# Ten batches of an MLP turned by VectorE blocks and SBUF transfers in place of TensorE transposes

## The chip, the cores and the metric

The kernel runs on one core of a Trainium2 chip. The metric is the device time of one execution in microseconds, and the median over the runs counts.

## The reference

The reference is one transformer block over 16 batches of 256 tokens with 256 features: modulated layer norm and self-attention with 16 heads, cross-attention to a context of 256 tokens, and an MLP of width 1024. All of it is fp32.

```python
x = x + gate_a[:, None] * attn_out          # self-attention
x = x + c_attn_out                          # cross-attention
x_norm2 = modulate(_ln(x), shift_m, scale_m)   # _ln(x) * (1 + scale_m) + shift_m
h = jax.nn.gelu(x_norm2 @ W_mlp1 + b_mlp1)
h = h @ W_mlp2 + b_mlp2
x = x + gate_m[:, None] * h
```

The change touches only the MLP's input: `x_norm2` must have the features on the partitions before it is multiplied by `W_mlp1`.

## The kernel before

The attention of all batches comes first and takes most of the time. It writes its result `x` to a DRAM tensor (`X2d`). The MLP then goes through the batches in order. Some of its first batches begin beside the end of the attention; from batch 3 on a loop at the end of the program (L1209 to L1234) drives it, and this loop is the place of the change.

Each matrix product is made of three fp32r products. Every operand is split into a rounded part (hi) and the rest (lo), and hi x hi, hi x lo and lo x hi are summed in PSUM.

A batch of the MLP goes in these steps:

- `mlp_load` (L804) reads `x` of the batch from DRAM, by SP's queue. `mlp_bias` (L812) adds the cross-attention's bias on GpSimd. `mlp_stats` (L815) takes mean and variance on VectorE, `pow` (L307) makes the reciprocal root on GpSimd, and `mlp_apply` (L819) writes the normalized rows `xn` on VectorE, tokens on partitions, in two instructions of 128x256.
- `mlp_T` (L833) turns `xn` by four TensorE transposes of 128x128 into PSUM (`psT_m`). VectorE scales and shifts them into SBUF (`xTf_m`, two instructions), ACT writes the same, rounded, to hi (two instructions), and VectorE subtracts hi to get lo. hi and lo lie in `Wkc` for even batches and `Wqc` for odd ones (`wkch`, `wkcl`, `wqch`, `wqcl` in the profile); these are weight tiles of the attention that are no longer needed.
- The width of 1024 is cut into four chunks c of 256. `mlp_first` (L857) makes one chunk in PSUM (`ph`, twelve matmuls of 128x256). `mlp_gelu` (L890) reads `ph` on ACT twice, once for the exact value `hf` and once for the rounded `hh` (two instructions each), and GpSimd subtracts them to `hl`. `mlp_second` (L907) multiplies the chunk by `W_mlp2` into PSUM (`st` or `s`, by the batch's parity; twelve matmuls) over all four chunks. After the last chunk VectorE multiplies by the gate (`mt`), adds the residual (`y`), and SP stores it.
- `mlp_gates` (L822) loads the gate's rows (`gm`), and `mlp_residual` (L828) prepares `xmg` on VectorE.

One turn of the loop is one chunk (b, c), and the text calls it so. TensorE gets, in this order: at c = 0 the four transposes of batch b+1, then `mlp_first` of the chunk two ahead, then `mlp_second` of the chunk before. So in (b, 0) it works on `ph` of (b, 2) and the last chunk of batch b-1, and `ph` of (b+1, 0), the first that needs hi and lo of batch b+1, comes in (b, 2).

The order on TensorE, VectorE, GpSimd and SP is the program's order (`keep_in_program_order`, L52); only ACT is left to a scheduler in the last part. Every instruction goes through the helper at L51, so nearly all rows of the profile have that line, and are told apart by their tiles.

Of the kernel before, what the change touches and what calls it, by code (L numbers as in the profile page):

```python
# [10 lines left out]
F32 = mybir.dt.float32  # L11
F32R = mybir.dt.float32r
AF = mybir.ActivationFunctionType
ALU = mybir.AluOpType
AX = mybir.AxisListType

P = 128
# [4 lines left out]
def pixart_block(  # L22
# [8 lines left out]
    B, N, H = x.shape  # L31
# [3 lines left out]
    NT = N // P  # L35
    KC = H // P
# [21 lines left out]
    ACT, DVE, POOL, SP = (InOrder(e, True) for e in (nc.scalar, nc.vector, nc.gpsimd, nc.sync))  # L58

    const = ctx.enter_context(tc.tile_pool(name="const", bufs=1))  # L60
    work = ctx.enter_context(tc.tile_pool(name="work", bufs=2))
# [6 lines left out]
    def ps_gen(name, tag=None):  # L68


        if tag is None and ps_turn[0] is not None:
            ps_turn[0] ^= 1
            tag = (SHORT, LONG)[ps_turn[0]]
        tag = tag or SHORT
        return psum.tile([P, 512], F32, tag=tag, name=name, bufs=2)
# [25 lines left out]
    def tok(ap, b):  # L101
        return ap[b].rearrange("(t p) h -> p t h", p=P)
# [18 lines left out]
    def wtile(name, c):  # L121
        return [const.tile([P, KC, c], F32R, name=f"{name}{s}") for s in ("h", "l")]

    Wq, Wk, Wv, Wp = [[wself[:, 4 * i:4 * i + 2], wself[:, 4 * i + 2:4 * i + 4]] for i in range(4)]
    Wqc = wtile("wqc", H)
    Wkc, Wvc, Wcp = wtile("wkc", H), wtile("wvc", H), wtile("wcp", H)
    cpT = const.tile([P, 12, B], F32, name="cpT")
    bqkv = const.tile([P, 6, B], F32, name="bqkv")
    sc1 = const.tile([P, 2, 2, B], F32, name="sc1")
    bT = const.tile([P, 32], F32, name="bT")  # L130
# [302 lines left out]
    def mm3_tok(dst, xT, t, W, kn=KC, start=True, stop=True):  # L433
        n = 0
        for k in range(kn):
            for a, b in ((xT[0], W[0]), (xT[0], W[1]), (xT[1], W[0])):
                PE.matmul(dst, a[:, k, t * P:(t + 1) * P], b[:, k],
                          start=(start and n == 0), stop=(stop and n == 3 * kn - 1))
                n += 1
# [134 lines left out]
    def bc_t(ap):  # L574
        return ap.unsqueeze(1).to_broadcast([P, NT, H])
# [113 lines left out]
    def side(home, r):  # L689
        return home[r] if isinstance(home, (list, tuple)) else home[:, r]  # L690
# [111 lines left out]
    M = {}  # L802

    def mlp_load(b):  # L804
        m = M[b] = M.get(b) or Box()
        if not hasattr(m, "h"):
            m.h, m.hT, m.kept = {}, {}, []
        m.xt = work.tile([P, NT, H], F32, tag="x" if b > 1 else "c", name=f"x2_{b}", bufs=5 if b > 1 else 2)
        SP.dma_start(m.xt, tok(X2d, b))
        m.ln = layernorm(lambda: m.xt, f"m{b}")  # L810

    def mlp_bias(b):  # L812
        POOL.tensor_tensor(M[b].xt, M[b].xt, bc_t(cb), ALU.add)

    def mlp_stats(b, power=False):  # L815
        M[b].ln.steps[0]()
        M[b].ln.steps[1](power)

    def mlp_apply(b):  # L819
        M[b].ln.steps[2]("dve")  # L820

    def mlp_gates(b):  # L822
        m = M[b]
        m.g = work.tile([P, 2, H], F32, tag="g", name=f"gm_{b}", bufs=3)
        SP.dma_start(m.g.rearrange("p a h -> p (a h)"),
                     gd[b, 2:4].rearrange("a h -> (a h)").partition_broadcast(P))

    def mlp_residual(b):  # L828
        m = M[b]
        m.xg = work.tile([P, NT, H], F32, tag="x1", name=f"xmg_{b}", bufs=7)  # L830
        DVE.tensor_tensor(m.xg, m.xt, bc_t(m.g[:, 1]), ALU.add)

    def mlp_T(b):  # L833

        m = M[b]
        pst = ps_gen(f"psT_m{b}", SHORT)
        for f in range(KC):
            for t in range(NT):
                PE.transpose(pst[:, f * N + t * P:f * N + (t + 1) * P],
                             m.ln.xn[:, t, f * P:(f + 1) * P], ident)  # L840
        y = work.tile([P, KC, N], F32, tag="y", name=f"xTf_m{b}", bufs=2)
        hi, lo = (Wkc, Wqc)[b % 2]
        for f in range(KC):
            DVE.tensor_scalar(y[:, f], pst[:, f * N:(f + 1) * N], sc1[:, 1, f, b:b + 1],
                              cpT[:, 6 + f, b:b + 1], ALU.mult, ALU.add)
        if b in E_['DV']:
            DVE.tensor_copy(hi, y)
        else:
            for f in range(KC):
                ACT.activation(hi[:, f], pst[:, f * N:(f + 1) * N], AF.Identity,  # L850
                               bias=cpT[:, 6 + f, b:b + 1], scale=sc1[:, 1, f, b:b + 1])
        DVE.tensor_tensor(lo, y, hi, ALU.subtract)
        m.xT = (hi, lo)

    NCH = NF // 2

    def mlp_first(b, c):  # L857

        ph = ps_gen(f"ph_{b}_{c}", LONG).rearrange("p (j n) -> p j n", j=2)
        for j in range(2):  # L860
            mm3(ph[:, j], W1, 2 * c + j, M[b].xT)
        M[b].h[c] = ph
# [27 lines left out]
    def mlp_gelu(b, c):  # L890
        ph = M[b].h.pop(c)
        homes = (("pt", 5), ("qkh", 3), ("qkl", 3))
        if b == 0 and c:
            homes = (("x1", 7),) + (homes[1:] if c < 3 else (("xTh", 5), ("xTl", 5)))
        hf, hh, hl = [work.tile([P, 2, N], t, tag=tag, name=f"{n}_{b}_{c}", bufs=bufs)
                      for n, t, (tag, bufs) in zip(("hf", "hh", "hl"), (F32, F32R, F32R), homes)]
        for dst in (hf, hh):
            if c in M[b].kept:
                ACT.activation(dst, ph, AF.Gelu_apprx_tanh)
                continue  # L900
            for j in range(2):
                f = BM1 + 2 * c + j
                ACT.activation(dst[:, j], ph[:, j], AF.Gelu_apprx_tanh, bias=bT[:, f:f + 1])
        POOL.tensor_tensor(hl, hf, hh, ALU.subtract)
        M[b].hT[c] = (hh, hl)

    def mlp_second(b, c):  # L907
        m = M[b]
        hT = m.hT.pop(c)
        if c == 0:  # L910
            m.po = [side((st, sp)[b % 2], t)[:, :H] for t in range(NT)]
        done = c == NCH - 1
        if done:
            t1 = work.tile([P, NT, H], F32, tag="t1", name=f"mt_{b}")
            y = work.tile([P, NT, H], F32, tag="x1", name=f"y_{b}", bufs=7)
        for t in range(NT):
            mm3_tok(m.po[t], hT, t, [W2[0][:, 2 * c:2 * c + 2], W2[1][:, 2 * c:2 * c + 2]],
                    kn=2, start=(c == 0), stop=done)
            if done and b == B - 1:
                DVE.tensor_tensor(t1[:, t], m.po[t], m.g[:, 0], ALU.mult)  # L920
                DVE.tensor_tensor(y[:, t], m.xg[:, t], t1[:, t], ALU.add)
                SP.dma_start(tok(out, b)[:, t], y[:, t])
        if done and b < B - 1:
            for t in range(NT):
                DVE.tensor_tensor(t1[:, t], m.po[t], m.g[:, 0], ALU.mult)
            DVE.tensor_tensor(y, m.xg, t1, ALU.add)
            SP.dma_start(tok(out, b), y)
# [6 lines left out]
    steps = {"x": mlp_load, "b": mlp_bias, "s": mlp_stats, "p": lambda b: M[b].ln.pow(), "a": mlp_apply,  # L934
             "r": mlp_residual, "g": mlp_gates, "T": mlp_T, "F": lambda j: mlp_first(j // NCH, j % NCH),
             "G": lambda j: mlp_gelu(j // NCH, j % NCH), "S": lambda j: mlp_second(j // NCH, j % NCH)}

    def tail_word(w):
# [96 lines left out]
    for i in range(3):  # L1035
        b = i if i < 2 else 0
        u = ahead_of_mlp(nu + i, b)
        u.T, u.ln = [], []
        if i < 2:
            u.ln = [layernorm(lambda b=b: M[b].xt, f"m{b}")]  # L1040
            u.T = [transposed(lambda u=u: u.ln[0].xn, f"m{b}", [sc1[:, 1, f, b:b + 1] for f in range(KC)],
                              bias=[cpT[:, 6 + f, b:b + 1] for f in range(KC)])]
# [153 lines left out]
    last, o, q = units[-1], units[-1].post, units[-2].post  # L1196
    chunks = [(b, c) for b in range(B) for c in range(NCH)]
    M[0].h[3] = tail[2].K.ps.rearrange("p (j n) -> p j n", j=2)
# [9 lines left out]
        done[w]() if w in done else tail_word(w)  # L1208
    for i, (b, c) in list(enumerate(chunks))[12:]:  # L1209
        ACT.on = i < E_['AP']  # L1210
        if i + 1 < len(chunks):
            mlp_gelu(*chunks[i + 1])
        if c == 0 and b < B - 1:
            mlp_T(b + 1)
        if i + 2 < len(chunks):
            mlp_first(*chunks[i + 2])
        mlp_second(*chunks[i - 1])
        ahead = b + 2 if b + 2 < B else None
        if c == 0 and ahead:
            mlp_bias(ahead)  # L1220
        if c == 1:
            if b + 1 < B:
                mlp_gates(b + 1)
            if ahead:
                mlp_stats(ahead)
            if b + 3 < B:
                mlp_load(b + 3)
        if c == 2 and ahead:
            M[ahead].ln.pow()
        if c == 3:  # L1230
            if ahead:
                mlp_apply(ahead)
            mlp_residual(b)
    mlp_second(*chunks[-1])  # L1234


# [46 lines left out]
```

## Time and profile before

| | before |
|---|---|
| median of 3 runs | 743.66 us (741.77 to 743.85) |
| profiled execution, its own time | 741.67 us |
| its span | 739.3 us |
| TensorE busy (PE) | 732.6 us, 99% |
| VectorE busy (DVE) | 572.3 us, 77% |
| ACT busy | 564.0 us, 76% |
| GpSimd busy (POOL) | 540.0 us, 73% |
| granted TensorE clock | 1.00 |

In the profile PE is TensorE's matmuls, PEld its weight loads, DVE is VectorE, POOL is GpSimd, and SPq is the queue of transfers that SyncE issues. A row of the timeline has the start and the length in us from the start of the span, the engine, the line, the operation, the tile written and the tiles read, their shapes, the number of instructions merged into the row, and in brackets the idle time of the engine before it and what ended it. A row of the chain of waits has the start, the length and the work that the end of the program hung on at that time. A row of the groups has the operation, the count, and behind the bar the busy time in us, the mean in ns of one instruction, and the idle time before them. The MLP's loop fills the span from about 560 us on.

### The profile page before, as it was taken

Reading aid. Unit: us, or ns where it says so; the run is one execution under the profiler, and the core shown is the slowest. Engines: PE = TensorE matmul, PEld = TensorE weight load, DVE = VectorE, ACT = ScalarE, POOL = GpSimd, SP = SyncE. Lnnn points to the kernel's source line nnn. Section 1 sums busy time; section 2 is a strip of 40 time slices with the busy share of each in tenths; the row PEclk is TensorE's granted clock in tenths of the full one; section 3 lists DMA queues with packets and bytes.
Section 4 is the critical chain, followed back from the end, with each engine's and each line's share of the span. In section 5 each row is a group of like instructions: output and inputs, shape, how many; then the busy total and the mean of one; then the engine's idle time right before and its main releaser. Section 6 shows DMA issues by size and latency. Waiting matters only on the chain.

```text
span 739.3 us, 25308 instructions
## 1 busy us (share of the span) xinstructions
PE 732.6 (99%) x10152; PEld 648.9 (88%) x10152; DVE 572.3 (77%) x1187; ACT 564.0 (76%) x979; POOL 540.0 (73%) x571
## 2 busy tenths in 40 slices
PE   9999999999999999999999999999999999999997
PEld 9878888888888888888888888888889999999997
DVE  4788898988889898888889898888726656666662
ACT  3278898888888888888888888898886666666663
POOL 6776687969687696968769798798647766666553
PEclk9999999999999999999999999999999999999999
DMA  6755445443544445354445545545113122221311
GB/s 193 214 151 152 132 129 141 128 131 93 170 120 135 135 135 145 95 160 130 133 136 147 154 124 163 137 142 150 58 61 106 51 72 71 61 86 44 86 51 37
DMA packets 89065, 87.98 MB, mean 119 GB/s; under 512 B 8626, under 2 KB 84692, under 8 KB 88948
## 3 DMA queue, kind: packets, MB, share of 16 engines
q1 hardware_dynamic: 88484, 85.58, 41.2%
q8 instruction: 80, 1.31, 0.7%
q0 software_dynamic: 192, 0.52, 0.3%
q14 instruction: 37, 0.30, 0.1%
q10 hardware_dynamic: 272, 0.26, 0.1%
HBM read 26.97 MB, written 8.46 MB: 48 GB/s over the span
## 4 chain that ended last, share of the span: by engine, by line
PE 95%; POOL 1%; DVE 1%; ACT 1%; issue 1%; DMA 0%; SPq 0%; POOLq 0%; ACTq 0%
PE s L51 18%; PE o L51 16%; PE st L51 16%; PE ph L51 11%; PE ps_q L51 5%; PE ps_qc L51 4%; PE ps_v_c L51 3%; PE ps_kc L51 3%; PE ps_P_s L51 3%; PE ps_k L51 3%; PE ps_P_c L51 2%; PE ps_v_s L51 2%; PE psT_q L51 1%; PE psT_m L51 1%; PE ps_h L51 1%; PE psA_s L51 1%
## 5 line engine op out<-in xcount | busy, mean ns | idle before, releaser
L51 DVE TENSOR_REDUCE mx<-s 128x2 f32<-128x512 f32 x504 | 324.6, 683 | 64.2 <-PE s L51 58.1
L51 ACT ACTIVATE pt<-st 128x1024 f32<-128x1024 f32 x252 | 258.9, 1027 | 16.6 <-PE st L51 10.5
L51 PE MATMUL s<-big 63*128 63x256 f32 (+1 forms) x1024 | 183.6, 297 | 0.1
L51 PEld LDWEIGHTS s<-big 63*128 63x128 f32 (+1 forms) x1024 | 133.3, 185 | 18.3 <-DVE l_kc L51 6.6
L51 PE MATMUL st<-big 64*128 64x256 f32 (+1 forms) x1024 | 134.3, 298 | 0.6 <-DMA big<-m 0.3
L51 POOL TENSOR_TENSOR hl<-hf,hh 128x512 fp32r<-128x512 f32 x64 | 84.9, 1329 | 64.6 <-ACT hh L51 64.6
L51 PE MATMUL o<-pt,v 128*32 128x256 f32 x2048 | 123.8, 382 | 0.0
L51 PEld LDWEIGHTS st<-big 64*128 64x128 f32 (+1 forms) x1024 | 96.0, 186 | 16.4 <-issue 13.2
L51 PEld LDWEIGHTS o<-pt,v 128*32 128x32 f32 x2048 | 60.0, 109 | 41.4
L51 ACT ACTIVATE hf<-ph,bT 128x256 f32<-128x256 f32 x114 | 47.8, 473 | 27.6 <-PE ph L51 27.6
L51 ACT ACTIVATE hh<-ph,bT 128x256 fp32r<-128x256 f32 x114 | 47.8, 471 | 22.5 <-PE s L51 11.8
L51 ACT COPY oT<-o 128x512 f32<-128x512 f32 x63 | 36.9, 586 | 33.2 <-PE o L51 33.2
L51 DVE TENSOR_SCALAR xn_m<-x,mv_m,rs_m 128x256 f32<-128x256 f32 x28 | 24.0, 900 | 32.1 <-POOL rs_m L51 32.1
L51 PE MATMUL st<-big,hh 128*128 128x256 f32 x256 | 46.7, 281 | 0.0
L51 PE MATMUL s<-big,hh 128*128 128x256 f32 x256 | 46.7, 281 | 0.0
L51 PE MATMUL ph<-wkch,wself 128*128 128x256 f32 x224 | 44.9, 284 | 0.0
L51 PE MATMUL ph<-wqch,wself 128*128 128x256 f32 x224 | 44.7, 284 | 0.0
L51 PE MATMUL ps_k<-xTh_s,wself 64*128 64x256 f32 (+1 forms) x232 | 43.7, 294 | 0.0
L51 POOL TENSOR_SCALAR xn_c<-c,mv_c,rs_c 128x256 f32<-128x256 f32 x32 | 38.9, 1226 | 1.7
L51 PE MATMUL ps_q<-xTh_s,wself 64*128 64x256 f32 (+1 forms) x240 | 39.7, 282 | 0.0
L51 PEld LDWEIGHTS s<-big,hh 128*128 128x128 f32 x256 | 39.0, 188 | 0.0
L51 PEld LDWEIGHTS st<-big,hh 128*128 128x128 f32 x256 | 39.0, 188 | 0.0
(244 smaller groups left out, 2517.1 us busy)
## 6 DMA issues: line engine op xcount, KB each, us to landing
big<-h_kc SPq DMA_DIRECT2D x64, 128.0 KB
big<-h_qc SPq DMA_DIRECT2D x64, 128.0 KB
big<-h_k SPq DMA_DIRECT2D x62, 128.0 KB
big<-h_q SPq DMA_DIRECT2D x62, 128.0 KB
big<-l_k SPq DMA_DIRECT2D x32, 128.0 KB
big<-l_q SPq DMA_DIRECT2D x32, 128.0 KB
g<-gd SPq DMA_DIRECT2D x16, 256.0 KB
c<-in_ctx_dram SPq DMA_DIRECT2D x16, 256.0 KB
```

The lines of the kernel that those rows point to most:

```text
L51: i = f(*a, **k)
```

## The change

For batches 6 to 15 (`TURN = 6`) TensorE no longer turns the rows. VectorE turns `xn` in blocks of 32x32 into a tile `z`, in two instructions. Four transfers on SP's queue, 64 KB each in runs of 512 bytes from SBUF to SBUF, then bring the blocks to their partitions in a tile `y` (`yT` in the profile). VectorE scales and shifts `y` back into `z` (two instructions), copies it rounded to hi, and subtracts to get lo. ACT no longer writes hi. The tokens of these batches come out in another order (block of 32, half, token in the block); GELU writes its result back in the old order, so the later steps see no difference.

So that the transfers have time, the steps of these batches are moved forward in the loop: the load to (b, 0) for batch b+3, the bias to (b, 2), the statistics to (b, 3) behind the residual, the reciprocal root of batch b+2 to (b, 0), the normalization and the turn to (b, 1). The scaling, copy and subtraction of batch b+1 stand in (b, 0), where the transposes stood. The lists of instructions of the two programs differ on TensorE in ten groups of four transposes that are gone, and in nothing else.

```diff
+    TURN = 6
+
+    def mlp_turn(b):
+        m = M[b]
+        m.z = work.tile([P, 4, KC, NT * 32], F32, tag="xn", name=f"z_{b}", bufs=3)
+        m.y = work.tile([P, 4, KC, NT * 32], F32, tag="y", name=f"yT_{b}", bufs=2)
+        for t in range(NT):
+            DVE.transpose(m.z[:, :, :, 32 * t:32 * t + 32].rearrange("p j k c -> p k j c"),
+                          m.ln.xn[:, t].rearrange("p (k c j) -> p k j c", k=KC, j=4))
+        for a in range(4):
+            SP.dma_start(m.y[:, a].rearrange("p k c -> p (k c)"),
+                         m.z[32 * a:32 * a + 32].rearrange("r j k c -> r j (k c)"))
+
+    def mlp_turned(b):
+        m = M[b]
+        hi, lo = m.xT = (Wkc, Wqc)[b % 2]
+        for f in range(KC):
+            DVE.tensor_scalar(m.z[:, :, f], m.y[:, :, f], sc1[:, 1, f, b:b + 1],
+                              cpT[:, 6 + f, b:b + 1], ALU.mult, ALU.add)
+        y = m.z.rearrange("p a k c -> p k a c")
+        hi, lo = [w.rearrange("p k (a c) -> p k a c", a=4) for w in (hi, lo)]
+        DVE.tensor_copy(hi, y)
+        DVE.tensor_tensor(lo, y, hi, ALU.subtract)
...
-                ACT.activation(dst[:, j], ph[:, j], AF.Gelu_apprx_tanh, bias=bT[:, f:f + 1])
+                src, to = ph[:, j], dst[:, j]
+                if b >= TURN:
+                    src = src.rearrange("p (a t c) -> p a t c", a=4, t=NT)
+                    to = to.rearrange("p (t a c) -> p a t c", a=4, t=NT)
+                ACT.activation(to, src, AF.Gelu_apprx_tanh, bias=bT[:, f:f + 1])
...
+        by_dma = [d if d < B and d >= TURN else None for d in range(b + 1, b + 4)]
+        by_pe = b + 2 if b + 2 < TURN else None
+        if c == 0 and by_dma[1]:
+            M[by_dma[1]].ln.pow()
         if i + 1 < len(chunks):
             mlp_gelu(*chunks[i + 1])
-        if c == 0 and b < B - 1:
-            mlp_T(b + 1)
+        if c == 0 and b + 1 < B:
+            (mlp_turned if by_dma[0] else mlp_T)(b + 1)
+        if c == 0 and by_dma[2]:
+            mlp_load(by_dma[2])
...
         if c == 1:
+            if by_dma[1]:
+                mlp_apply(by_dma[1])
+                mlp_turn(by_dma[1])
             if b + 1 < B:
                 mlp_gates(b + 1)
-            if ahead:
-                mlp_stats(ahead)
-            if b + 3 < B:
-                mlp_load(b + 3)
...
+        if c == 2:
...
+            if by_dma[2]:
+                mlp_bias(by_dma[2])
         if c == 3:
...
             mlp_residual(b)
+            if by_dma[2]:
+                mlp_stats(by_dma[2])
```

More of the change, by code (lines that the diff above doesn't have):

```diff
@@ L1217, in pixart_block @@
         mlp_second(*chunks[i - 1])
-        ahead = b + 2 if b + 2 < B else None
-        if c == 0 and ahead:
-            mlp_bias(ahead)
+        if c == 0 and by_pe:
+            mlp_bias(by_pe)
         if c == 1:
+            if by_dma[1]:
+                mlp_apply(by_dma[1])
+                mlp_turn(by_dma[1])
             if b + 1 < B:
                 mlp_gates(b + 1)
-            if ahead:
-                mlp_stats(ahead)
-            if b + 3 < B:
-                mlp_load(b + 3)
-        if c == 2 and ahead:
-            M[ahead].ln.pow()
+            if by_pe:
+                mlp_stats(by_pe)
+        if c == 2:
+            if by_pe:
+                M[by_pe].ln.pow()
+            if by_dma[2]:
+                mlp_bias(by_dma[2])
         if c == 3:
-            if ahead:
-                mlp_apply(ahead)
+            if by_pe:
+                mlp_apply(by_pe)
             mlp_residual(b)
+            if by_dma[2]:
+                mlp_stats(by_dma[2])
     mlp_second(*chunks[-1])
```

## The prediction

> **What bounds the kernel now.** I read the page's busy shares first, then the busy time by stage, then the chain of waits for the stage that the change touches.
>
> ```profile
> PE 732.6 (99%) x10152; PEld 648.9 (88%) x10152; DVE 572.3 (77%) x1187; ACT 564.0 (76%) x979; POOL 540.0 (73%) x571
> ```
> ```profile
> 640.00:660.00 20.00, 20.00 (x172) 20.00 (x171) 13.94 (x22) 13.24 (x32) 12.81 (x12) 1.00 0.19 57
> ```
> ```profile
> 619.09 0.44 PE psT_m L51 x4
> 619.53 1.43 PE ph L51 x12
> ...
> 629.46 1.42 PE st L51 x12
> 630.88 0.44 PE psT_m L51 x4
> 631.32 1.43 PE ph L51 x12
> ```
>
> In the stage (columns: window, its length, then PE, PEld, DVE, ACT, POOL busy, granted clock, DMA share, GB/s) PE is busy 20.00 of 20.00 us at clock 1.00, while DVE, ACT and POOL are busy 13 to 14. The chain holds nothing but PE there: one batch is eight groups of twelve matmuls at 1.42 and one group of four transposes at 0.44. From 619.53 to 631.32 is 11.79 us, the period of a batch. Another engine matters only if it makes PE wait.
>
> **What goes.**
>
> ```profile
> L51 PE MATMUL psT_m<-ident,xn_m 128*128 128x128 f32 x40 | 6.0, 271 | 0.0
> L51 ACT ACTIVATE wqch<-psT_m,cpT,sc 128x256 fp32r<-128x256 f32 x10 | 5.1, 562 | 3.8 <-DVE xTf_m L51 3.8
> ```
>
> Forty transposes (from 600 us on) are the ten batches 6 to 15, the ones that TURN takes. What they cost the path is not 271 ns each, since they overlap, but their 0.44 us slot in the chain: 10 x 0.44 = 4.4 us. Nothing else moves in PE's instruction list; the other groups keep their order. The period would be 11.79 - 0.44 = 11.35. ACT loses two writes of hi per batch (2 x 0.56), which were not on the path.
>
> **What comes.** One period of VectorE and GpSimd before:
>
> ```profile
> 640.36 1.81 DVE L51 TENSOR_SCALAR xn_m<-x,mv_m,rs_m 128x256 f32<-128x256 f32 x2 [2.58 <-POOL rs_m L51]
> 642.09 0.68 DVE L51 TENSOR_TENSOR xmg<-x,gm 128x512 f32<-128x512 f32 x1
> 643.14 0.99 DVE L51 TENSOR_SCALAR xTf_m<-psT_m,sc,cpT 128x256 f32<-128x256 f32 x2 [0.38 <-PE psT_m L51]
> 645.29 1.38 DVE L51 TENSOR_TENSOR wqcl<-xTf_m,wqch 128x512 fp32r<-128x512 f32 x1 [1.15 <-ACT wqch L51]
> 646.59 0.74 DVE L51 TENSOR_TENSOR mt<-s,gm 128x256 f32<-128x256 f32 x2
> 647.37 1.33 DVE L51 TENSOR_TENSOR y<-xmg,mt 128x512 f32<-128x512 f32 x1
> 648.61 0.74 DVE L51 BATCH_NORM_STATS2 st_m<-x 128x6 f32<-128x256 f32 x2
> 649.28 0.29 DVE L51 BATCH_NORM_AGGREGATE mv_m<-st_m 128x2 f32<-128x6 f32 x2
> ```
> ```profile
> 640.73 1.29 POOL L51 TENSOR_TENSOR hl<-hf,hh 128x512 fp32r<-128x512 f32 x1 [0.40 <-ACT hh L51]
> 644.81 1.30 POOL L51 TENSOR_TENSOR x<-x,cb 128x512 f32<-128x512 f32 x1
> 646.85 1.29 POOL L51 TENSOR_TENSOR hl<-hf,hh 128x512 fp32r<-128x512 f32 x1 [0.73 <-ACT hh L51]
> 649.74 1.28 POOL L51 TENSOR_TENSOR hl<-hf,hh 128x512 fp32r<-128x512 f32 x1 [1.59 <-ACT hh L51]
> 642.86 0.36 PE L51 MATMUL ph<-wkch,wself 128*128 128x256 f32 x1
> ```
> ```profile
> 640.69 1.48 DVE L51 TENSOR_SCALAR xn_m<-x,mv_m,rs_m 128x256 f32<-128x256 f32 x1
> ...
> 663.93 0.41 DVE L51 TENSOR_SCALAR xn_m<-x,mv_m,rs_m 128x256 f32<-128x256 f32 x1 [2.58 <-POOL rs_m L51]
> ...
> 728.84 0.69 DVE L51 TENSOR_TENSOR y<-xmg,mt 128x512 f32<-128x512 f32 x1
> ```
>
> The last three rows are one half of xn beside an hl, one half of xn alone and one y alone. Alone a half took 0.41; beside hl it took 1.48 and ended 0.15 after the hl of 640.73: a DVE instruction that meets hl waits until hl is through. So did y (1.33 against 0.69) and, behind the x of 644.81, the subtraction (1.38). I carry this into the sum: meeting hl costs up to its 1.29.
>
> Durations of the new work, per batch:
>
> ```profile
> L51 POOL TENSOR_TENSOR rs_m<-rs_m,mhalf 128x2 f32<-128x2 f32 x10 | 7.1, 707 | 0.8
> L51 ACT ACTIVATE hh<-ph,bT 128x256 fp32r<-128x256 f32 x90 | 37.7, 470 | 18.1 <-PE st L51 9.8 <-PE s L51 8.3
> L51 DVE TENSOR_SCALAR xn_m<-x,mv_m,rs_m 128x256 f32<-128x256 f32 x20 | 18.1, 946 | 25.8 <-POOL rs_m L51 25.8
> L51 DVE CAST big<-w 128x512 fp32r<-128x512 f32 x1 | 0.4, 419 | 0.0
> ```
> ```profile
> 302.73 2.48 SPq L51 DMA_DIRECT2D big<-h_qc  x4
> 33.18 0.59 SPq L51 DMA_DIRECT2D big<-m  x1
> 36.61 0.36 PE L51 MATMUL st<-big 64*128 64x256 f32 x1
> PE st L51 <- DMA big<-m: 0.3, 1, 0.3
> ```
>
> Two 32x32-block transposes of 128x256: no such row. Nearest is a one-input instruction of that shape, 0.41; the mean of those that met GpSimd, 0.95, is the other end. I take 0.42 each, 0.85 together, since nothing says that they meet hl (bound 1.9). Two scalings, now from SBUF: 0.41 each, and less than the 0.50 from PSUM. The copy to hi: 0.42. The subtraction: 0.69, or 1.38 behind hl.
>
> Four transfers of 64 KB on SP's queue: four regroupings of the same kind took 2.48 to issue, 0.62 each, so the last starts 1.86 after the first. The one transfer on which PE was seen to wait was issued at 33.18 and released PE at 36.6: 3.4. Sum 5.25 from the transposes' end to the landing; ends 4.0 (shorter landing) and 7.0 (four that queue). Behind them on SP stand gm and the next x, each needed over a period later, so that 2.5 us there costs nothing. The scaling waits for the landing; behind it on DVE stand mt and y, whose PSUM is written again only two batches on. GELU now writes runs of 32:
>
> ```profile
> 308.18 0.58 ACT L51 COPY v<-ps_v_c 128x512 f32<-128x512 f32 x1
> 306.42 0.59 ACT L51 COPY y_as<-psT_as 128x512 f32<-128x512 f32 x1
> ```
>
> The copy to v writes runs of 16 and takes no longer than the contiguous one, so I leave GELU at 0.47 an instruction; ACT has 6 us in 20 to spare if not. The moved pow (0.7 and a shorter addition) and bias fit between the hl of GpSimd (below), and the load only comes earlier.
>
> **Does VectorE still keep up?** Its list becomes: mt, y, xn, transposes of batch b+2; xmg, stats (under the transfers); scalings, copy, subtraction of b+2; mt of the next. That is a loop with the transfers inside. Alone: 0.74 + 0.69 + 0.82 + 0.85 + 5.25 + 0.82 + 0.42 + 0.69 = 10.3, against 11.35. So 1.05 us are left for meetings with hl. I walked it through. t = 0 is the start of ph of (b,2), 642.86 before; hl stood at 646.85 and 649.74, which is 4.0 and 6.9; one per chunk of 2 x 1.42 gives 1.1, 4.0, 6.9, 9.7 and from 12.5 again, 1.29 each, since ACT's part before it waits for PE's groups.
> - mt waits for PE's eighth group: 3.1 to 3.85. y to 4.55 (it begins before hl, and pushes it to 5.85). xn to 6.3, transposes to 7.1.
> - Transfers land at 12.4. xmg and stats are over by 10.5 (stats waits for the bias behind the hl of 6.9: 8.2 + 1.3 = 9.5).
> - First scaling 12.8; the second waits for hl, 13.9; copy 14.3; subtraction 15.0. PE needs hi and lo at 11.35 + 4 x 1.42 = 17.0: 2.0 early.
> - The next mt was ready at 14.45, so it is 0.55 late, but y then stands behind hl as it would have anyway: transposes end at 18.85, which is 7.5 in its own period. Landing 12.8; both scalings behind hl, 14.3; subtraction 15.4. The next round comes out at 15.4 again: it settles, 1.6 us before PE needs it.
>
> The hl that y pushes to 5.85 is read by PE at 3 x 2.84 + 1.42 = 9.9. So PE waits for nothing, and the whole slot is gained. With transposes and transfers together 7.1 instead of 6.1 the same walk gives the subtraction's end at 15.7, 16.0, 18.3: it slips past 17.0 in the third round. Seven us is the threshold.
>
> The Trainium skill (VectorE: DVE Perf Modes, The three transpose paths) gives 311 ns for a 128x128 bf16 block transpose on VectorE against 390 on TensorE; doubled for 256 columns that is an estimate of 0.62 each, 1.24 together, and no run here shows it. By it the sum is 6.5, still under seven.
>
> The skill's DMA: Bandwidth & Descriptors, Anatomy of one DMA, puts the fixed part at about 2.0 us; by it the landing would be 4.0 after the transposes and the subtraction some 1.4 earlier. The trace's 3.4 decides here.
>
> **The sum.** The profiled execution took 741.67 (span 739.3); 741.67 - 4.4 = 737.3. The median of the runs is 743.66, 2.0 above that execution; 743.66 - 4.4 = 739.3 (0.6%).
>
> **Rivals.**
> 1. Slower: the VectorE loop becomes the bound. Place: the first ph of each batch waits for lo. Point: transposes, transfers and waits for hl push the loop past 11.35 and use up the 1.6 us. If y, one xn, one scaling and the subtraction all fell behind hl (+0.64, +1.0, +1.1, +0.69), the loop is 13.7; with about two thirds of that, 12.7, nine loops give 9 x 1.35 = 12.1, less 1.6, less 4.4: +6.1, 749.8. For: three of those four meetings are in the rows of before. Against: the walk shows they do not add, since hl's beat is PE's. 0.20.
> 2. No change: the loop at 11.95, by transposes of 0.95 each (+1.05) and 0.6 of waits for hl; 9 x 0.6 - 1.6 = 3.8 against 4.4: 743.1. 0.13.
> 3. Forecast, 739.3: 0.67.
>
> A measurement of this kernel tells about 0.3%, 2.2 us, from no change, so 741.4 to 745.9 is "same". The forecast's own range is 737 to 741.4 (the scatter of the runs before, 2.1 us). The whole range goes to 745.9, where rival 2 ends; what is left out is rival 1.
>
> **What would show it.** Right: in the chain ten groups of 0.44 gone, PE still 20.00 of 20.00, a period of 11.35; transposes near 0.42; lo's end over a microsecond ahead of the first ph that uses it. Wrong: idle time of PE before ph whose releaser is DVE lo; z waiting on the transfers over 7 us after the transposes; GELU above 0.47. A period over 11.79 with DVE without idle time is rival 1.

## The result, and the profile after

| | before | after |
|---|---|---|
| median | 742.41 us (6 runs) | 737.47 us (6 runs) |
| ratio, 95% interval | | 0.993 (0.9915 to 0.9946) |
| the same again, beside other experiments | 741.61 us (11 runs) | 737.57 us (5 runs), 0.9945 (0.9931 to 0.9959) |
| profiled execution, span | 739.3 us | 735.6 us |

The kernel became 4 to 5 us faster; 4.4 had been forecast. The six runs before include the three that gave the 743.66 from which the prediction counted; 742.41 - 4.4 is 738.0. The chain of waits after, from the same part of the MLP's loop (columns: start, length, work):

```profile
635.37 1.42 PE s L51 x12
636.78 1.42 PE ph L51 x12
638.20 1.42 PE s L51 x12
639.62 1.42 PE ph L51 x12
641.04 1.42 PE s L51 x12
642.45 1.42 PE ph L51 x12
643.87 1.42 PE s L51 x12
645.28 1.42 PE ph L51 x12
646.70 1.42 PE st L51 x12
```

The pieces of 0.44 are gone and nothing has taken their place: from 635.37 to 646.70 is 11.33 us, against 11.79. The busy time of the same stage (window, length, PE, PEld, DVE, ACT, POOL, granted clock, DMA share, GB/s) shows who paid:

```profile
640.00:660.00 20.00, 20.00 (x172) 20.00 (x171) 15.89 (x30) 11.91 (x30) 13.29 (x13) 1.00 0.32 92
```

TensorE is busy throughout, as before. VectorE went from 13.94 to 15.89 us in 20, ACT from 13.24 to 11.91, and the DMA engines from 19% to 32%. One round of VectorE's loop, then SP's transfers inside it and the first matmuls that need the result:

```profile
637.31 1.16 DVE L51 STREAM_TRANSPOSE z<-xn_m 128x256 f32<-128x256 f32 x2
638.41 1.12 DVE L51 TENSOR_TENSOR xmg<-x,gm 128x512 f32<-128x512 f32 x1
640.71 0.75 DVE L51 BATCH_NORM_STATS2 st_m<-x 128x6 f32<-128x256 f32 x2 [1.18 <-POOL x L51]
641.38 0.30 DVE L51 BATCH_NORM_AGGREGATE mv_m<-st_m 128x2 f32<-128x6 f32 x2
642.63 0.74 DVE L51 TENSOR_SCALAR z<-yT,sc,cpT 128x256 f32<-128x256 f32 x2 [0.96 <-DMA yT<-z]
643.48 1.45 DVE L51 CAST wqch<-z 128x512 fp32r<-128x512 f32 x1
644.96 0.69 DVE L51 TENSOR_TENSOR wqcl<-z,wqch 128x512 fp32r<-128x512 f32 x1
645.57 0.75 DVE L51 TENSOR_TENSOR mt<-s,gm 128x256 f32<-128x256 f32 x2
646.35 1.67 DVE L51 TENSOR_TENSOR y<-xmg,mt 128x512 f32<-128x512 f32 x1
647.94 0.73 DVE L51 TENSOR_SCALAR xn_m<-x,mv_m,rs_m 128x256 f32<-128x256 f32 x2
648.59 1.17 DVE L51 STREAM_TRANSPOSE z<-xn_m 128x256 f32<-128x256 f32 x2
```
```profile
638.50 2.49 SPq L51 DMA_DIRECT2D yT<-z  x4
```
```profile
647.95 0.28 PE L51 MATMUL ph<-wqch,wself 128*128 128x256 f32 x1
```

```profile
643.35 1.29 POOL L51 TENSOR_TENSOR hl<-hf,hh 128x512 fp32r<-128x512 f32 x1 [0.26 <-ACT hh L51]
646.18 1.29 POOL L51 TENSOR_TENSOR hl<-hf,hh 128x512 fp32r<-128x512 f32 x1 [1.54 <-ACT hh L51]
```

VectorE waits for the transfers (0.96 before the scaling, released by DMA), but it ends lo at 645.65 (644.96 + 0.69), and TensorE begins the product that reads hi and lo at 647.95. These 2.3 us are the margin of this round; in the ten rounds of the profile it is 1.6 to 2.6. The wait is real and costs nothing. The last two rows are the hl of GpSimd beside which the copy (1.45) and y (1.67) ran.

### The profile page after: what moved, and what is told of

It reads as the page before. It is cut to its first block, busy times and chain, and to the rows that moved or that the text cites. A ratio compares the mean times of both kernels' runs of the same rounds, so it can differ in the third digit from the quotient of the medians.

```text
span 735.6 us, 25307 instructions
## 1 busy us (share of the span) xinstructions
PE 728.9 (99%) x10112; PEld 644.8 (88%) x10112; DVE 584.8 (79%) x1217; ACT 555.5 (76%) x959; POOL 546.3 (74%) x571
## 4 chain that ended last, share of the span: by engine, by line
PE 93%; DVE 3%; POOL 2%; issue 1%; ACT 1%; DMA 1%; SPq 0%; POOLq 0%; ACTq 0%
PE s L51 18%; PE o L51 16%; PE st L51 16%; PE ph L51 10%; PE ps_q L51 5%; PE ps_qc L51 4%; PE ps_v_c L51 3%; PE ps_kc L51 3%; PE ps_P_s L51 3%; PE ps_k L51 2%; PE ps_v_s L51 2%; PE ps_P_c L51 2%; DVE mx L51 1%; PE psT_q L51 1%; PE ps_h L51 1%; PE psA_s L51 1%
## 5 line engine op out<-in xcount | busy, mean ns | idle before, releaser
L51 POOL TENSOR_TENSOR hl<-hf,hh 128x512 fp32r<-128x512 f32 x64 | 87.0, 1361 | 52.9 <-ACT hh L51 52.8
L51 PE MATMUL ps_P_s<-wself,xTh_as 64*128 64x256 f32 x256 | 39.1, 282 | 0.0
```

The source lines that it names most:

```text
L51: i = f(*a, **k)
```

## The experiments

**Is it TensorE's slot?** The transposes were put back beside the new turn, in a new function `idle_turn` whose four `PE.transpose` write a PSUM tile that nobody reads (its body is left out here):

```diff
             (mlp_turned if by_dma[0] else mlp_T)(b + 1)
+            if by_dma[0]:
+                idle_turn(b + 1)
...
```

> The changed kernel with the four TensorE transposes put back at their old place for batches 6 to 15, into a PSUM tile that nothing reads. Theory (the gain is TensorE's slot): each batch gets its 0.44 us slot back, a period of 11.77 in the chain instead of 11.33, 737.5 + 4.4 = 741.9 us. Rival (the gain comes from the steps moved forward, or from ACT's two writes of hi that are gone): nothing of that is undone here, so the time stays at 737.5.

Measured: 741.72 us against 741.73 for the kernel before beside it, ratio 1.0004 (0.9991 to 1.0016). Its chain:

```profile
642.27 1.42 PE s L51 x12
643.68 0.44 PE psI_m L51 x4
644.12 1.43 PE ph L51 x12
```

The slot of 0.44 is back, the next one stands 11.79 later (655.47), and the gain is gone, although the new order, the lighter ACT and all of VectorE's new work stayed.

**Is it the order of the steps?** The order alone, with the old turn for all batches:

```diff
-                if b >= TURN:
+                if False:
...
-            (mlp_turned if by_dma[0] else mlp_T)(b + 1)
+            mlp_T(b + 1)
...
-                mlp_turn(by_dma[1])
```

> The new order of the steps (load, bias, statistics, root and normalization moved forward) with the old turn by TensorE for all batches, ACT writing hi again. Theory (TensorE's slot): period 11.79, the time of the kernel before, 742.4. Rival (the order brings the gain): 737.5 to 738.5.

Measured: 742.41 us, ratio 1.0009 (0.9997 to 1.0021). In its chain the pieces of 0.44 stand 11.79 apart (632.76 and 644.55). The order is worth nothing by itself; it is there to give the transfers time.

**How much time do they have?** Eight transfers, then sixteen, in place of four; the bytes are the same:

```diff
-            SP.dma_start(m.y[:, a].rearrange("p k c -> p (k c)"),
-                         m.z[32 * a:32 * a + 32].rearrange("r j k c -> r j (k c)"))
+            for k in range(KC):
+                SP.dma_start(m.y[:, a, k], m.z[32 * a:32 * a + 32, :, k])
```

> The changed kernel with eight transfers of 32 KB (runs of 256 bytes) in place of four of 64 KB; bytes and places are the same. Theory (VectorE's loop has a limit at TensorE's period): the profile after has 2.49 us for four issues, so the landing comes 2.5 later, 6.7 after the transposes' end. The loop alone becomes 0.75 + 0.69 + 0.72 + 1.17 + 6.66 + 0.74 + 0.43 + 0.69 = 11.85 and, with 0.5 to 1.5 of waits for hl, 12.3 to 13.3 against 11.33; nine loops less some 2.3 of slack give 744 to 753, and TensorE idle before ph until lo. Rival (transfers are hidden anyway): 737.5, no idle time.

Measured: 755.8 us, ratio 1.0176 (1.0153 to 1.0199), a little above the expected range. In most of the loop the chain has left TensorE; a stretch of it, and two rows of TensorE:

```profile
651.55 0.60 SPq L51
652.15 0.04 issue
652.20 1.90 DMA yT<-z
...
654.29 0.42 DVE z L51
...
654.81 0.44 DVE wqch L51
655.25 0.02 issue
655.27 1.64 DVE wqcl L51
```
```profile
655.38 0.36 PE L51 MATMUL ph<-wqch,wself 128*128 128x256 f32 x1 [1.42 <-DVE wqch L51]
656.96 0.58 PE L51 MATMUL ph<-wqcl,wself 128*128 128x256 f32 x1 [1.22 <-DVE wqcl L51]
```

SP issues one transfer after the other, the last lands 1.90 after its issue, VectorE runs on it at once, and TensorE stands before ph until hi and then lo are written. In all ten rounds TensorE waits there. This is the first rival of the prediction, at the place it named. The first of the two scalings in three rounds one after the other:

```profile
639.44 0.41 DVE L51 TENSOR_SCALAR z<-yT,sc,cpT 128x256 f32<-128x256 f32 x1 [5.47 <-DMA yT<-z]
653.55 0.41 DVE L51 TENSOR_SCALAR z<-yT,sc,cpT 128x256 f32<-128x256 f32 x1 [4.41 <-DMA yT<-z]
667.02 0.41 DVE L51 TENSOR_SCALAR z<-yT,sc,cpT 128x256 f32<-128x256 f32 x1 [4.44 <-DMA yT<-z]
```

These rounds take 14.1 and 13.5 us, and the nine from the first scaling at 610.79 to the one at 734.73 take 13.8 on average; 12.3 to 13.3 had been expected, on 11.85 for the loop alone. What came on top can be read in single rounds. In the one from 653.55, lo took 1.64 and y 1.77 beside work of GpSimd, 0.69 each alone, which adds 2.0. In the one from 639.44 a scaling, y and xn lost 2.1 in this way, and the eight issues took 5.78 in place of 5.09. Nine loops of 13.8 - 11.33, less 2.3 of margin, are 20 us over the changed kernel. This profiled execution, the longest of the five, took 759.18, 21.5 over the changed kernel (0.9945 x 741.73 = 737.7); the median is 18 over it.

> The same with sixteen transfers of 16 KB (runs of 128 bytes). Theory (VectorE's loop sets the period): the landing comes 7.4 later than with four, loop 16.8 alone and about 17.5 with waits, 9 x (17.5 - 11.33) - 2.3 = 53 over the changed kernel, 785 to 797, and a period in the chain that is VectorE's. Rival (hidden): 737.5.

Here each half was cut once more, into 32 tokens. Measured: 796.0 us (2 runs), ratio 1.0725 (1.0698 to 1.0752), inside the expected range. SP's row shows the issue that sets it; in the nine rounds it takes 10.2 to 11.2:

```profile
657.67 11.16 SPq L51 DMA_DIRECT2D yT<-z  x16
```

**Where is the threshold?** Six transfers, two of 64 KB and four of 32 KB:

```diff
-            SP.dma_start(m.y[:, a].rearrange("p k c -> p (k c)"),
-                         m.z[32 * a:32 * a + 32].rearrange("r j k c -> r j (k c)"))
+            if a < 2:
+                SP.dma_start(m.y[:, a].rearrange("p k c -> p (k c)"),
+                             m.z[32 * a:32 * a + 32].rearrange("r j k c -> r j (k c)"))
+            else:
+                for k in range(KC):
+                    SP.dma_start(m.y[:, a, k], m.z[32 * a:32 * a + 32, :, k])
```

> The changed kernel with six transfers: two of 64 KB, and the other two cut in halves. Theory (VectorE's loop with the threshold of the prediction, seven us from the transposes' start to the landing): the profile after has 1.17 + 4.16 = 5.3 there, two more issues make it 6.6; the loop alone is 10.6 against 11.33, so TensorE still waits for little or nothing: ratio to the changed kernel within 0.3%, 0.993 to 0.996 of the kernel before. Rival (waits for hl come on top of the loop as they did with eight transfers, 13.5 against 11.85 alone, some 1.6): the loop is 12.2, nine loops less 2.3 of slack make it 5 to 6 us slower than the changed kernel, a ratio of 1.000 to 1.002.

Measured: 737.69 us, ratio 0.9949 (0.9937 to 0.9961), the changed kernel's 0.9945 beside it. VectorE's rows:

```profile
648.91 1.16 DVE L51 STREAM_TRANSPOSE z<-xn_m 128x256 f32<-128x256 f32 x2
...
655.29 1.14 DVE L51 TENSOR_SCALAR z<-yT,sc,cpT 128x256 f32<-128x256 f32 x1 [0.20 <-DMA yT<-z]
```

From the transposes' start to the scaling that needs the last transfer it is 6.4 us, the next such scaling comes 11.3 later (666.60), and TensorE waits for nothing. The ten rounds have 6.2 to 6.9, and one 7.4, which the margin took up. With eight the same distance was 8.5 (645.83 to 654.29) and 7.75 (659.95 to 667.70), about 7.5 to 8.7 in the ten rounds, and TensorE waits in each. So for a loop that goes on, the threshold lies between some 6.4 and 7.5. The rival, that waits for hl come on top in full, would have cost 5 to 6 us and is ruled out here.

**What got lost at the start?** In the profile after, the chain between batch 4's and batch 5's transposes is longer than before:

```profile
584.34 0.44 PE psT_m L51 x4
...
593.82 2.69 DVE xn_m L51 x2
596.51 0.04 issue
596.55 0.55 PE psT_m L51 x3
```

Before, the same two pieces were 11.79 apart:

```profile
583.73 0.44 PE psT_m L51 x4
...
595.52 0.44 PE psT_m L51 x4
```

Now it is 12.2 (596.55 - 584.34). The normalization of batch 5 takes 2.69 and not 1.81, and beside it GpSimd now runs the moved bias of batch 6 and then an hl:

```profile
593.75 1.30 POOL L51 TENSOR_TENSOR x<-x,cb 128x512 f32<-128x512 f32 x1
595.01 1.34 POOL L51 TENSOR_TENSOR hl<-hf,hh 128x512 fp32r<-128x512 f32 x1
```

The bias was put one chunk earlier:

```diff
+            if b == 3:
+                mlp_bias(by_dma[2])
...
-            if by_dma[2]:
+            if by_dma[2] and b > 3:
                 mlp_bias(by_dma[2])
```

> The changed kernel with the bias of batch 6 one chunk earlier, in (3, 1) in place of (3, 2). In the profile after, that bias stands on GpSimd beside the normalization of batch 5 (2.69 us in place of 1.81), and TensorE's transposes of batch 5 wait for it. Theory: this wait of about 0.4 us goes, the chain from batch 4's transposes to batch 5's is 11.79 again in place of 12.2; the time falls by 0.4, less than the interval can tell. Rival (the wait comes from elsewhere): the chain stays at 12.2.

Measured: 736.69 us, ratio 0.9938 (0.9924 to 0.9953), against 737.57 for the changed kernel. The two intervals overlap, so the time does not settle it; the chain does:

```profile
583.82 0.44 PE psT_m L51 x4
...
595.61 0.44 PE psT_m L51 x4
```

It is 11.79 again. This version has the lowest median of the versions that do all the work, by an amount that these runs cannot tell from nothing.

**Is there more to win?** The turn left out of the kernel before:

```diff
-        pst = ps_gen(f"psT_m{b}", SHORT)
-        for f in range(KC):
+        if b < 6:
+            pst = ps_gen(f"psT_m{b}", SHORT)
+        if b >= 6:
+            pst = m.ln.xn.rearrange("p t h -> p (t h)")
+        for f in range(KC if b < 6 else 0):
             for t in range(NT):
...
```

> The kernel before with the turn left out for batches 6 to 15: no transposes, VectorE and ACT read xn itself, so these rows are not turned. It has no transposes on VectorE and no transfers. Theory (TensorE's slot is all there is to win): period 11.34, the same time as the changed kernel or some 0.4 below it, 0.993 of the kernel before. Rival (the changed kernel still pays something in the loop): clearly below the changed kernel, 0.990 or less.

Measured: 736.74 us, ratio 0.9935 (0.9921 to 0.9948). Its period is 11.33 (634.36 to 645.69 in its chain). As far as these runs can tell, leaving the turn out altogether gains no more than moving it did: it is 0.8 us below the changed kernel with intervals that overlap, and level with the one with the earlier bias.

> The changed kernel itself, beside the others on one chip: 0.993 of the kernel before, 4.4 us from TensorE's slots less 0.4 at batch 5.

Measured: 737.57 us, 0.9945 (0.9931 to 0.9959).

**What does a block turn take?**

```diff
-            DVE.transpose(m.z[:, :, :, 32 * t:32 * t + 32].rearrange("p j k c -> p k j c"),
-                          m.ln.xn[:, t].rearrange("p (k c j) -> p k j c", k=KC, j=4))
+            out_ = m.z[:, :, :, 32 * t:32 * t + 32].rearrange("p j k c -> p k j c")
+            if t == 0:
+                DVE.transpose(out_, m.ln.xn[:, t].rearrange("p (k j c) -> p k j c", k=KC, j=4))
+            else:
+                in_ = m.ln.xn[:, t].rearrange("p (k c j) -> p k j c", k=KC, j=4)
+                for k in range(KC):
+                    DVE.transpose(out_[:, k], in_[:, k])
```

> One look at what a 32x32-block turn on VectorE takes. In the changed kernel the first of the two (t = 0) reads its input in contiguous runs in place of every fourth element, which leaves those rows' features in another order; the second (t = 1) is cut into two of 128x128. If the stride of 16 bytes is what makes 128x256 take 618 ns and not the 420 predicted, the contiguous one takes some 420; if it is the turn's own rate, it stays at 618. The two halves tell the fixed part: 309 each if there is none (0.62 together), some 380 each with a fixed part near 0.15. The time as a whole stays within the slack, 737.

Measured: 737.71 us (one run; 742.33 before). The groups by shape, this kernel's two rows first, then the changed kernel's:

```profile
L51 DVE STREAM_TRANSPOSE z<-xn_m 128x128 f32<-128x128 f32 x20 | 6.6, 365 | 0.0
L51 DVE STREAM_TRANSPOSE z<-xn_m 128x256 f32<-128x256 f32 x10 | 4.3, 432 | 0.0
```
```profile
L51 DVE STREAM_TRANSPOSE z<-xn_m 128x256 f32<-128x256 f32 x20 | 11.6, 618 | 0.0
```

Reading every fourth element costs 618 ns against 432 for contiguous runs. Two halves of 128 take 0.73 us together, so cutting it up only adds, an estimate of 0.11 for each further instruction (2 x 365 - 618).

## Why the prediction was right, point by point

- **The slot.** 0.44 per batch, ten times. The period fell from 11.79 to 11.33, putting the transposes back undid the whole, and leaving the turn out gained no more. The mean of 271 ns for one transpose would have given 10.8 us; the slot in the chain was the right reading.
- **The sum.** 4.4 was forecast, 4.9 and 4.0 were measured between the medians of two sets. The time that was forecast, 739.3, came out 1.8 too high, of which 1.3 is the median of three runs from which it was counted. The chain explains 4.0: the 0.4 at batch 5 was not foreseen. The prediction said that the moved bias fits between the hl of GpSimd. In the steady loop it does; at the one seam where batch 5 still goes through TensorE it stood beside the normalization, and the earlier bias took the wait away.
- **The block turn.** Forecast 0.42 each from a one-input row, measured 0.62: the step was under-sized by half. The row it was taken from read contiguous data, and contiguous turns did take 0.43. So the sign "transposes near 0.42" did not appear; the margin paid for it. The Trainium skill's figure for bf16 (VectorE: DVE Perf Modes, The three transpose paths), doubled to an estimate of 0.62, came out right here by luck: this is fp32 with a strided input, and with contiguous runs 0.62 would have been too high.
- **The transfers.** Forecast 5.25 from the transposes' end to the landing, measured 4.16 (638.47 to 642.63). The issue was right (2.49 for four against 2.48). The landing was over-sized: 3.4 from the start of the issue was one transfer of 8 KB at the attention's start, where SP had issued eleven others in the seven us ahead of it (whether they delayed it is not shown); here the last of the four began at about 638.50 + 3 x 0.62 = 640.4 and was used 2.3 later, and in the kernel with eight it took 0.60 of issue and 1.90. The Trainium skill's 2.0 us of fixed cost (DMA: Bandwidth & Descriptors, Anatomy of one DMA), which that section fits to transfers issued by GpSimd and not by SP, was the nearer one, and the sentence "the trace's 3.4 decides" chose wrongly.
- **The two errors partly cancel.** The transposes took 0.3 more and the transfers 1.1 less: together 6.1 was forecast and 5.3 measured, 5.2 to 6.5 in the ten rounds. The walk said that lo would be 1.6 us early; it is 2.3 early in the round shown and 1.6 in the tightest. That the larger error lay on the slow side was luck; it left more margin than forecast.
- **Meetings with hl.** The rule held: the copy took 1.45 beside hl and 0.43 alone. The walk had y and both scalings behind hl. y did stand behind it, but of the scaling, the copy and the subtraction only one met it in each round: the scaling in three of the ten, the copy in four, the subtraction in three.
- **GELU.** 471 and 470 ns after, 470 and 472 before: runs of 32 cost nothing.
- **The rivals.** Seven us as the threshold lies inside 6.4 to 7.5 as measured. Beyond it, with eight transfers, the first rival's sign appeared: TensorE idle before ph until VectorE's lo. "No change" by transposes of 0.95 did not come about.

## What to carry to other kernels

Where one engine is busy without a gap, price a removed step by its slot in the chain, not by the length of its instructions. Work that was moved to other engines with a longer path cost nothing here as long as the loop that it forms there, transfers and waits and all, was shorter than the period of the bound engine. Add up that loop and keep the margin in view, for beyond it each microsecond was paid once per round. The number of transfers, not their bytes, filled the loop here: each cost some 0.6 us of issue on one queue, with 64, 32 or 16 KB, and the gate's rows and x, 256 KB each, took 0.59 and 0.39. The runs got shorter as the transfers got more (512, 256, 128 bytes), and no run changed one without the other.

## What the hardware showed beyond that

The granted clock was 1.00 in all of the MLP's stages of the kernel before, and of the kernel after but for the last (0.91 from 720 us on, where the program ends). In the kernel with sixteen transfers, where TensorE stands idle for part of every round, it was lower in each stage from 620 to 760 us, 0.78 to 0.91; two of them:

```profile
640.00:660.00 20.00, 15.84 (x107) 15.37 (x106) 9.54 (x24) 6.83 (x17) 7.67 (x8) 0.78 0.27 62
680.00:700.00 20.00, 16.34 (x123) 15.97 (x122) 8.34 (x16) 8.52 (x21) 8.70 (x8) 0.91 0.24 58
```

With eight transfers it was 0.91 or 0.92 in three of seven stages and 0.99 or 1.00 in the others, so some idle time alone does not settle it: from 700 to 720 us TensorE was busy 17.41 of 20 at 1.00, from 620 to 640 it was busy 17.59 at 0.91. What lowers the clock was not tested, and whether it lengthens those rounds is open: their chain runs over SP, the transfers and VectorE.
